# Layer 0, step one in source order with in-place tiles; four of nine channel blocks stored in one pixel order and gathered for the right-hand side

## The chip, the cores and the metric

The kernel runs on one NeuronCore of one Trainium2 chip. The metric is the device time of one launch in microseconds, from three runs of the same program, and beside them one execution was recorded by the hardware profiler. The core has five instruction queues: PE (matmuls; its weight loads, PEld, overlap them), DVE (vector), ACT (scalar, activation functions), POOL (GpSimd) and SP (here it only issues transfers). Transfers (DMAs) are issued from SP, ACT or POOL and carried out by 16 shared DMA engines.

## What is computed

Four residual layers act on an image batch of 8 x 56 x 56 pixels x 192 channels. Only layer 0 is touched by the change. It is a gated token mixer: two projections `q` and `v` to 576 channels are multiplied, the product is convolved along the width with one set of 576 Toeplitz filters and along the height with another, the sum is gated by a third projection `p`, and projected back to 192 channels.

```python
p = silu(x @ p_w.T + p_b)
q = silu(x @ q_w.T + q_b)
v = silu(x @ v_w.T + v_b)
...
qv = q * v
o1 = _toeplitz(qv.reshape(b * h, w, D1), a1).reshape(b, h, w, D1)
o2 = _toeplitz(transpose(qv, (0, 2, 1, 3)).reshape(b * w, h, D1), a2)
...
return (p * (o1 + o2)) @ o_w.T + o_b
```

`x` is group-normalised before it enters, and the result is added to the un-normalised `x`. Everything is float32.

## The kernel before

Layer 0 runs in two steps, with HBM between them.

**Step one** (lines 1319 to 1362 drive it; `layer0_qv`, line 374, is its body) makes `qv` for all eight images. An image lies in SBUF as 128 partitions: the upper and lower 64 partitions hold the two halves of the image (s = 0 and 1), 64 channels to a half, three channel groups j, 1568 pixels each. Per image there are 14 turns (`PH`), each on two pixel rows of either half, 112 pixels, and in a turn the 576 output channels are taken in two pieces of 288 (n). For each piece: 12 matmuls (2 projections x 3 j x 2 halves; each shows as four records of 288 columns, since float32 is passed four times), then for either half one DVE addition of the bias out of PSUM (line 393, 576 elements for q and v together), one ACT Silu (line 394), and one DVE multiplication q*v into a tile `qv` (line 395). After a turn's pieces, SP writes each half's product to HBM **twice**: to `left` (line 398, one DMA, rows of a channel block ordered by pixel row h, content along w) and to `right` (line 403, two DMAs, rows ordered by pixel column w, content along h). Channels are stored in nine blocks of 64 (`NSUB`), so every piece that is written is a run of 64 floats, 256 bytes: 1008 runs in each `left` DMA, 504 in each `right` DMA, and there are 224 and 448 of these DMAs.

Between turns `between[i]` runs small steps of other work: the Toeplitz coefficients (`toeplitz_rows`; PE, DVE), the Toeplitz matrices themselves (128 DMAs in all, `row` and `zeros`, lines 296 and 301, each 9 rows of 14,336 bytes from HBM to HBM, issued from ACT's queue), a bias-and-mask table for layer 1, and at turn 4 the statistics and the normalisation of the next image (`layer0_in`: 12 `bn_stats`, a group sum through PE, ACT Sqrt, and line 371, which writes a normalised copy `xn` of the whole image on DVE). The order of instructions on each engine is the tile framework's scheduler's. `act` has 4 buffers, `qv` 3, `x0` and `xn0` 2 each, PSUM 4 tiles of two banks.

**Step two** (`layer0_mix`, line 521) walks over 72 blocks (8 images x 9 channel blocks). For each it loads two operands into 128 partitions (`layer0_block`, line 409): `lt`, whose even partitions hold 64 rows of the Toeplitz matrix and whose odd ones hold the 64 rows of `left`; and `rt`, the same from `right` with the places swapped, so that one matmul with 128 contraction rows adds both convolutions. Each operand is 128 rows of 14,336 bytes, one DMA on SP's queue (line 417). They have two buffers each (`raws`, bufs=2), so the load of a block is issued when the last copy out of the block two before has been made. From `lt`, POOL copies slices of eight channels (`lc`, line 425), from `rt` DVE and ACT take turns (`rc`); PE multiplies (`op`, line 433), DVE and ACT take the result out (`o`, line 590). Blocks 0 to 3, 4 to 7 and 8 of an image form three passes; the gating and output projection of one pass (lines 438 to 519) is spread between the products of the next. Around block 4 to 5 of each image SP also stores the finished image (line 538) and loads a new one (line 528).

Every DMA is tied to one of eight completion semaphores of the hardware queues (SP and ACT share them), and an issue waits until the DMA that used its semaphore before has landed: at most eight are outstanding.

Of the kernel before, what the change touches and what calls it, by code (L numbers as in the profile page):

```python
# [10 lines left out]
F32 = mybir.dt.float32  # L11
AF = mybir.ActivationFunctionType
ALU = mybir.AluOpType
# [4 lines left out]
B, H, W, C = 8, 56, 56, 192  # L18
NT = H * W
HC = 96  # L20
TT = 392
NTT = NT // TT
D1 = 576
DCH = [(0, 128), (128, 128), (256, 128), (384, 128), (512, 64)]
NSUB = D1 // 64

PASSES = [((0, 1), (0, 1, 2, 3)), ((2, 3), (4, 5, 6, 7)), ((4,), (8,))]
DPERM = [128 * c + 32 * (s % 4) + i for cs, ss in PASSES[:2] for s in ss for c in cs for i in range(32)]
# [22 lines left out]
QR = 56 * 64  # L51
# [11 lines left out]
NH = NT // 2  # L63
NTH = NH // TT
PH = NPAIR // 2
# [24 lines left out]
def kernel(ctx: ExitStack, tc: tile.TileContext, a: dict, out: bass.AP):  # L90
    nc = tc.nc
    nimg = a["x"].shape[0]

    const = ctx.enter_context(tc.tile_pool(name="const", bufs=1))
    dram = ctx.enter_context(tc.tile_pool(name="dram", bufs=1, space=DRAM))
# [17 lines left out]
    gmath = resident("gmath")  # L113
# [7 lines left out]
    eps5 = const.tile([128, 1], F32, name="eps5")  # L121
# [12 lines left out]

    coef = [dram.tile([NSUB, 111, 64], F32, name=f"coef{i}") for i in range(2)]
    none = dram.tile([QR], F32, name="none")
    left, right = (dram.tile([(nimg * W + 64) * NSUB, QR], F32, name=n) for n in ("left", "right"))
    qv_row = lambda b, s: (b * NSUB + s) * W
    toep_row = lambda s: nimg * NSUB * W + 64 * s
    x1 = [dram.tile([C, NT], F32, name=f"x1_{b}") for b in range(nimg)]  # L140
    bmask = dram.tile([8, 128, 3 * 4 * 2 * WN], F32, name="bmask")
    wgd = dram.tile([128, 3, 3 * C], F32, name="wgd")
# [11 lines left out]
    def gn_piece(st, x, t):  # L154

        for j in range(3):
            nc.vector.bn_stats(st[:, j, t], x[:, j, bass.ts(t, TT)])

    def gn_aggregate(st, mv):
        nc.vector.bn_aggr(mv, st.rearrange("p j t s -> p (j t s)"))  # L160
# [29 lines left out]
    def run(steps):  # L190
        for _ in steps:
            pass
# [34 lines left out]
    def toeplitz_rows(psum, pool, rows):  # L227
# [16 lines left out]
        k = 1  # L244
        while k < 55:
            n = min(k, 55 - k)
# [9 lines left out]
        for i in range(2):  # L256
            m = f"m{i + 1}_"
            h = pool.tile([32, 111], F32, name=f"h{i}")
# [3 lines left out]
        for l in range(3):  # L262
            yield
            for i in range(2):
                ps = psum.tile([128, 2, 512], F32, name="hps", tag="qv")
# [6 lines left out]
        for c, (d0, M) in enumerate(DCH):  # L272
            yield
            cos = []
            for i in range(2):
                ps = psum.tile([128, 2, 512], F32, name="aps", tag="qv")
# [7 lines left out]
            for i in range(2):  # L284
                ps = psum.tile([128, 2, 512], F32, name="cps0", tag="qv")
# [4 lines left out]
        zero = pool.tile([128, QR // 128], F32, name="zero", bufs=1)  # L290
        nc.gpsimd.memset(zero, 0.0)
        nc.scalar.dma_start(none.rearrange("(p n) -> p n", p=128), zero)
        parts = [z[toep_row(0):].rearrange("(s k) n -> k s n", k=64) for z in (left, right)]

        def row(i, w0):
            nc.scalar.dma_start(
                parts[i][w0], coef[i][:, 55 - w0:111 - w0].rearrange("s l d -> s (l d)")
            )

        def zeros(i, k):  # L300
            nc.scalar.dma_start(parts[i][k], none.partition_broadcast(NSUB))

        rows += [lambda i=i, k=k: zeros(i, k) for i in range(2) for k in range(W, 64)]
        rows += [lambda i=i, w0=w0: row(i, w0) for i in range(2) for w0 in range(W)]
# [48 lines left out]
    def layer0_load(b, pool):  # L353
        x = pool.tile([128, 3, NH], F32, name="x0")
        nc.gpsimd.dma_start(x, a["x"][b])
        return x

    def layer0_in(b, x, pool, psum):

        sc, sh = scsh[:, 0, b:b + 1], scsh[:, 1, b:b + 1]  # L360
        st = pool.tile([128, 3, NTH, 6], F32, name="gh_st")
        for t in range(NTH):
            gn_piece(st, x, t)
        mv = pool.tile([128, 1, 2], F32, name="gh_mv")
        gn_aggregate(st, mv[:, 0])
        run(gn_finish(mv, sc, sh, pool, psum, "qv"))
        xn = pool.tile([128, 3, NH], F32, name="xn0")
        n = NH if b else TT
        for t in range(NH // n):
            ts = bass.ts(t, n)  # L370
            nc.vector.tensor_scalar(xn[:, :, ts], x[:, :, ts], sc, sh, ALU.mult, ALU.add)
        return xn

    def layer0_qv(b, xn, pool, psum, w_qv, b_qv, between):

        lv, rv = (
            z[qv_row(b, 0):qv_row(b, 0) + NSUB * W].rearrange("(s h) (w d) -> s h w d", h=W, d=64) for z in (left, right)
        )
        for i in range(PH):
            qv = pool.tile([2 * W, 2, D1], F32, name="qv", bufs=3)  # L380
            for n in range(2):
                ns = slice(n * D1 // 2, (n + 1) * D1 // 2)
                ps = [psum.tile([2 * W, 2, 512], F32, name=f"qv{s}", tag="qv") for s in range(2)]
                for which in range(2):
                    for j in range(3):
                        for s in range(2):
                            nc.tensor.matmul(  # L387
                                ps[s][:, which, 0:D1 // 2], xn[64 * s:64 * s + 64, j, bass.ts(i, 2 * W)],
                                w_qv[64 * s:64 * s + 64, j, which, ns], start=(j == 0), stop=(j == 2),
                            )  # L390
                for s in range(2):
                    act = pool.tile([2 * W, 2, D1 // 2], F32, name="act", bufs=4)
                    nc.vector.tensor_tensor(act, ps[s][:, :, 0:D1 // 2], b_qv[:, :, ns], ALU.add)  # L393
                    nc.scalar.activation(act, act, AF.Silu)  # L394
                    nc.vector.tensor_tensor(qv[:, s, ns], act[:, 0], act[:, 1], ALU.mult)
            for s in range(2):
                h0 = H // 2 * s + 2 * i
                nc.sync.dma_start(
                    lv[:, h0:h0 + 2].rearrange("s h w d -> (h w) s d"),
                    qv[:, s].rearrange("t (s d) -> t s d", d=64),  # L400
                )
                for r in range(2):
                    nc.sync.dma_start(
                        rv[:, :, h0 + r].rearrange("s w d -> w s d"),
                        qv[r * W:(r + 1) * W, s].rearrange("w (s d) -> w s d", d=64),
                    )
            for step in between[i]:
                step()

    def layer0_block(b, s, raws):  # L410


        raw = [raws.tile([128, QR], F32, name=n) for n in ("lt", "rt")]
        rows_qv, rows_t = qv_row(b, s), toep_row(s)
        for t, z, even, odd in ((raw[0], left, rows_t, rows_qv), (raw[1], right, rows_qv, rows_t)):
            one = z[even:even + 64]
            nc.sync.dma_start(
                t, bass.AP(one.tensor, one.offset, [[QR, 64], [(odd - even) * QR, 2], [1, QR]]),
            )
        return raw  # L420

# [900 lines left out]
    with ExitStack() as st:  # L1322
        pool = st.enter_context(tc.tile_pool(reuse_waits="tile", name="qv", bufs=2))
        psum = st.enter_context(tc.tile_pool(reuse_waits="tile", name="qvp", bufs=4, space=PSUM))
        w_qv = resident("w_qv", nc.scalar, pool)
        b_qv = pool.tile([2 * W, 2, D1], F32, name="b_qv", bufs=1)
        nc.scalar.dma_start(b_qv.rearrange("p a d -> p (a d)"), a["b_qv"].partition_broadcast(2 * W))
        tz = st.enter_context(tc.tile_pool(reuse_waits="tile", name="tz", bufs=2))
        x = layer0_load(0, pool)
        xn = layer0_in(0, x, pool, psum)  # L1330
        rows, masks = [], []
        coefs, bias = toeplitz_rows(psum, tz, rows), build_bias_mask(psum, tz, masks)
        centred = layer1_weights(tz, psum)

        def pop(todo, n=1):
            for _ in range(min(n, len(todo))):
                todo.pop(0)()

        for b in range(nimg):

            between = {i: [lambda i=i: pop(rows, 2 if i % 3 == 1 else 1)] for i in range(PH)}
            if b == 0:
                for i in range(PH):
                    between[i].insert(0, lambda: [next(coefs, None) for _ in range(2)])
                between[10].append(lambda: next(bias, None))
            elif b == 1:
                between[6].append(lambda: next(bias, None))
                between[12].append(lambda: pop(masks))
            elif b == 2:
                for i in range(6):  # L1350
                    between[2 * i].append(lambda: next(centred, None))
            if b:
                between[9].append(lambda: pop(masks))
            ahead = []
            if b + 1 < nimg:
                x = layer0_load(b + 1, pool)
                between[4].append(lambda: ahead.append(layer0_in(b + 1, x, pool, psum)))
            layer0_qv(b, xn, pool, psum, w_qv, b_qv, between)
            xn = ahead[0] if ahead else None
        pop(rows, len(rows))  # L1360
        pop(masks, len(masks))
    with ExitStack() as st:
        pool = st.enter_context(tc.tile_pool(reuse_waits="tile", name="mix", bufs=2))
# [7 lines left out]
        images, x = ExitStack(), []  # L1371
# [312 lines left out]
```

## Time and profile before

| what | before |
|---|---|
| median of 3 runs | 5757.5 us (5750.73 to 5760.37) |
| the profiled execution: device time, span | 5770.6 us, 5768.8 us |
| mean granted TensorE clock | 0.957 |
| busy share of the span | PE 90%, DVE 58%, ACT 38%, POOL 25% |
| step one: first and last matmul record of line 387 | 28.6 and 846.7 us |
| step one: last store issued (line 403) | 857.2 us |
| step two: last load of an operand issued (line 417) | 1987.0 us |
| transfers: packets, of them under 512 B | 721,922 and 486,376 |

The page's header gives the span; the table of groups gives for each source line how often an instruction ran, the mean of one, and what the engine waited for in front of it; a window row gives the busy time of each engine in a stretch, the clock granted to TensorE, the mean busy share of the 16 DMA engines and what they moved. Step one takes the first 15% of the span and step two the next 20%; the other three layers follow, and the change does not touch them.

### The profile page before, as it was taken

How to read it: one execution, taken by the hardware profiler on the slowest of the kernel's cores; microseconds unless marked ns; L12 is line 12 of the kernel's file. 1: busy time of each engine (PE TensorE's matmuls, PEld its weight loads, DVE VectorE, ACT ScalarE, POOL GpSimd, SP SyncE). 2: the span in 40 equal slices, each digit the busy share in tenths (PEclk: the TensorE clock that was granted, in tenths of full speed). 3: DMA queues.
4: the chain of work that ended last, by engine and by line, in shares of the span. 5: the costliest groups of instructions: out<-in, count | busy, mean ns of one | idle time of the engine just before them, and what ended most of it. 6: DMA issues, size and time to landing. Idle time of an engine off the chain costs nothing. (4 is left out here: it accounts for less than half of the span.)

```text
span 5768.8 us, 116138 instructions
## 1 busy us (share of the span) xinstructions
PE 5181.2 (90%) x50342; PEld 3376.1 (59%) x50342; DVE 3336.5 (58%) x4710; ACT 2169.1 (38%) x2908; POOL 1420.2 (25%) x1107
## 2 busy tenths in 40 slices
PE   6898998999899979999997989999788798999999
PEld 4568765666666645555554657676344597444444
DVE  5777774555555546566665868888778202433331
ACT  2333443333333423333332004555476400433333
POOL 2100004444444424433342013333101101100100
PEclk8999999999999989999998989999899899999999
DMA  6888986776677633222222866666687598212211
GB/s 179 204 211 216 206 182 258 264 264 258 247 262 264 222 92 82 69 75 76 69 65 76 260 235 218 227 232 209 160 232 215 222 328 295 78 62 77 76 41 26
DMA packets 721922, 1013.94 MB, mean 176 GB/s; under 512 B 486376, under 2 KB 645444, under 8 KB 694644
## 3 DMA queue, kind: packets, MB, share of 16 engines
q1 hardware_dynamic: 706352, 940.12, 52.4%
q0 software_dynamic: 8512, 40.62, 2.1%
q10 hardware_dynamic: 6548, 25.78, 1.4%
q8 instruction: 396, 6.49, 0.5%
q14 instruction: 114, 0.93, 0.0%
HBM read 676.92 MB, written 345.97 MB: 177 GB/s over the span
## 5 line engine op out<-in xcount | busy, mean ns | idle before, releaser
L387 PE MATMUL qv<-w_qv_sb,xn 64*112 64x288 f32 x5376 | 711.3, 421 | 48.6 <-DVE act L393 45.4
L425 POOL COPY lc<-lt 128x896 f32<-128x896 f32 (+1 forms) x320 | 552.5, 1751 | 640.9 <-PE op L433 543.1
L387 PEld LDWEIGHTS qv<-w_qv_sb,xn 64*112 64x112 f32 x5376 | 558.5, 182 | 195.5 <-DVE act L393 58.1
L394 ACT ACTIVATE act<-act 112x576 f32<-112x576 f32 x448 | 300.6, 683 | 466.8 <-DVE act L393 427.4
L433 PE MATMUL op<-rc,lc 128*56 128x56 f32 x9216 | 339.1, 221 | 102.1 <-POOL lc L425 64.9
L433 PEld LDWEIGHTS op<-rc,lc 128*56 128x56 f32 x9216 | 307.8, 135 | 177.9 <-POOL lc L425 103.5
L1289 PE MATMUL ph<-y,w_sb 64*128 64x392 f32 x2304 | 397.7, 497 | 6.5 <-ACT hid L1293 6.5
L1300 PE MATMUL po<-hid,w_sb 128*64 128x392 f32 x2304 | 386.3, 494 | 0.0
L393 DVE TENSOR_TENSOR act<-qv,b_qv 112x576 f32<-112x576 f32 x448 | 320.7, 752 | 92.7 <-PE qv L387 92.4
L1307 DVE TENSOR_TENSOR x<-x,z 128x392 f32<-128x392 f32 x96 | 67.0, 698 | 524.2 <-ACT z L1305 524.2
L425 ACT COPY rc<-rt 128x896 f32<-128x896 f32 (+1 forms) x160 | 256.3, 1606 | 249.7 <-PE op L433 227.2
L805 PE MATMUL qk_ps<-xr,wg 64*96 64x392 f32 x1536 | 334.2, 538 | 1.8 <-DVE xr L752 1.7
L1016 PE MATMUL cv<-zc,wt 128*128 128x224 f32 x1536 | 313.6, 356 | 24.2 <-DMA zc<-pd 24.2
L1016 PEld LDWEIGHTS cv<-zc,wt 128*128 128x128 f32 x1536 | 291.0, 190 | 67.5 <-issue 51.2
L1289 PEld LDWEIGHTS ph<-y,w_sb 64*128 64x128 f32 x2304 | 220.0, 188 | 175.9 <-issue 25.5
L445 PE MATMUL pj<-xn,w_p_sb 64*128 64x392 f32 x1536 | 309.8, 511 | 12.4 <-DVE xn L533 8.2
L1190 PE MATMUL cps<-zc,wt 128*128 128x224 f32 x1536 | 300.2, 356 | 18.2 <-DMA zc<-zd 16.8
L1190 PEld LDWEIGHTS cps<-zc,wt 128*128 128x128 f32 x1536 | 289.6, 189 | 28.7 <-issue 21.3
L466 PE MATMUL y<-pp,w_o_sb 128*64 128x392 f32 x1536 | 285.9, 501 | 4.8 <-DVE x L474 4.1
L459 DVE TENSOR_TENSOR pp<-pp,ot 128x784 f32<-128x784 f32 x128 | 124.2, 970 | 284.8 <-ACT pp L450 272.9
L1300 PEld LDWEIGHTS po<-hid,w_sb 128*64 128x64 f32 x2304 | 162.7, 137 | 213.8 <-issue 213.8
L1031 POOL TENSOR_TENSOR rows<-rows,loc 128x896 f32<-128x896 f32 x96 | 220.8, 2300 | 261.7 <-ACT rows L1027 201.9
(233 smaller groups left out, 8895.1 us busy)
## 6 DMA issues: line engine op xcount, KB each, us to landing
lt<-left SPq DMA_DIRECT2D x72, 1792.0 KB
rt<-right SPq DMA_DIRECT2D x72, 1792.0 KB
left<-qv SPq DMA_DIRECT2D x224, 252.0 KB
right<-qv SPq DMA_DIRECT2D x448, 126.0 KB
wt<-in_band_dram SPq DMA_DIRECT2D x23, 2048.0 KB
wt<-in_band_dram SPq DMA_DIRECT2D x11, 4096.0 KB
zc<-pd SPq DMA_DIRECT2D x187, 232.0 KB
pd<-pt SPq DMA_DIRECT2D x7, 5568.0 KB
```

The source lines that it names most:

```text
L387: nc.tensor.matmul(ps[s][:, which, 0:D1 // 2], xn[64 * s:64 * s + 64, j, bass.ts(i, 2 * W)], w_qv[64 * s:64 * s + 64, j, which, ns], start ...
L393: nc.vector.tensor_tensor(act, ps[s][:, :, 0:D1 // 2], b_qv[:, :, ns], ALU.add)
L394: nc.scalar.activation(act, act, AF.Silu)
L425: copy(c[:, 0:nu], raw.rearrange("p (w u d) -> p u d w", u=nu, d=64 // nu)[:, :, d0:d0 + 8])
L433: nc.tensor.matmul(op[64 * u:64 * u + W, i, :], lc[:, u, i], rc[:, u, i], start=True, stop=True)
L445: nc.tensor.matmul(ps[0:M, s, 0:TT], w_p[64 * s:64 * s + 64, j, d0:d0 + M], xn[64 * s:64 * s + 64, j, ts], start=(j == 0), stop=(j == 2),)
L466: nc.tensor.matmul(y[64 * s:64 * s + 64], w_o[0:M, c, 64 * j:64 * j + 64], pp[0:M, s], start=(c == gated[0][0]), stop=(c == gated[-1][0]),)
L805: nc.tensor.matmul(in_pairs(ps[s]), wg[64 * s:64 * s + 64, j, c0:c0 + HC], in_slots(xr[64 * s:64 * s + 64], (3 * g + j) * GW), start=(j == ...
L1016: nc.tensor.matmul(dst, wt[:, c4 + i, 128 * q:128 * q + 128], zc[:, :, c4 + i, q:q + NPAIR], start=(q == 0), stop=(q == 1),)
L1190: nc.tensor.matmul(dst.rearrange("p (b n) -> p b n", n=NPAIR), wt[:, c4 + i, q * OP:(q + 1) * OP], zc[:, :, c4 + i, q:q + NPAIR], start=(q ...
L1289: nc.tensor.matmul(ps[:, s, 0:TT], w0[64 * s:64 * s + 64, j, m * 128:(m + 1) * 128], y[64 * s:64 * s + 64, j, ts], start=(j == 0), stop=(j ...
L1300: nc.tensor.matmul(ps[64 * s:64 * s + 64], w1[:, m, 64 * j:64 * j + 64], hid[:, m, s], start=(m == 0), stop=(m == 5),)
```

## The change

- **Order.** Step one is recorded in a manual schedule: PE, ACT, DVE and POOL run their instructions in the order of the source. SP stays with the scheduler. The steps between are spread over 28 half turns; the statistics of the next image come one `bn_stats` at a time from the eighth half turn on.
- **In place.** The normalised image overwrites `x` (no `xn`); for images 1 to 7 this is done on POOL in four pieces of 1176 elements per partition. q*v overwrites its own `act` tile (no `qv` tile); `act` has 14 buffers. The multiplication comes one half turn late, for half s = 0 on DVE, for s = 1 on POOL.
- **Pieces.** A turn's channels are cut at a block border: 320 (blocks 0 to 4) and 256 (blocks 5 to 8). Each piece is stored as soon as it is multiplied, so a turn's half has two `left` DMAs (560 and 448 runs of 256 bytes) and four `right` DMAs.
- **Kept blocks.** `right` holds only the even channel blocks, five of nine (`KEPT`): its DMAs carry 168 or 112 runs. For an odd block, `rt` is filled by two DMAs: 64 Toeplitz rows of 14,336 bytes, and a gather from `left` of 64 columns x 56 rows, 3,584 runs of 256 bytes.
- **Queue.** The 128 Toeplitz DMAs are issued from SP instead of ACT.

```diff
+KEPT = (NSUB + 1) // 2
...
-    left, right = (dram.tile([(nimg * W + 64) * NSUB, QR], F32, name=n) for n in ("left", "right"))
+    left, right = (
+        dram.tile([nimg * W * k + 64 * NSUB, QR], F32, name=n) for n, k in (("left", NSUB), ("right", KEPT))
+    )
...
         def row(i, w0):
-            nc.scalar.dma_start(
+            nc.sync.dma_start(
                 parts[i][w0], coef[i][:, 55 - w0:111 - w0].rearrange("s l d -> s (l d)")
             )
...
-            nc.scalar.dma_start(parts[i][k], none.partition_broadcast(NSUB))
+            nc.sync.dma_start(parts[i][k], none.partition_broadcast(NSUB))
...
+        for t in range(NTH):
+            xs = x[:, :, bass.ts(t, TT)]
+            (nc.gpsimd if b else nc.vector).tensor_scalar(xs, xs, sc, sh, ALU.mult, ALU.add)
...
+        def multiply(i, s0, s1, acts):
+            n = 64 * (s1 - s0)
+            for s in range(2):
+                eng = (nc.vector, nc.gpsimd)[s]
+                eng.tensor_tensor(acts[s][:, 0, 0:n], acts[s][:, 0, 0:n], acts[s][:, 1, 0:n], ALU.mult)
+            for s in range(2):
+                h0 = H // 2 * s + 2 * i
+                qv = acts[s][:, 0, 0:n].rearrange("t (s d) -> t s d", d=64)
+                nc.sync.dma_start(lv[s0:s1, h0:h0 + 2].rearrange("s h w d -> (h w) s d"), qv)
+                kept = range(s0 + s0 % 2, s1, 2)
+                for r in range(2):
+                    nc.sync.dma_start(
+                        rv[kept[0] // 2:kept[-1] // 2 + 1, :, h0 + r].rearrange("s w d -> w s d"),
+                        qv[r * W:(r + 1) * W, kept[0] - s0:kept[-1] + 1 - s0:2],
+                    )
+
         for i in range(PH):
-            qv = pool.tile([2 * W, 2, D1], F32, name="qv", bufs=3)
-            for n in range(2):
+            for at, (s0, s1) in enumerate(((0, 5), (5, NSUB))):
...
+                acts = [pool.tile([2 * W, 2, 320], F32, name="act", bufs=14) for _ in range(2)]
                 for s in range(2):
-                    act = pool.tile([2 * W, 2, D1 // 2], F32, name="act", bufs=4)
-                    nc.vector.tensor_tensor(act, ps[s][:, :, 0:D1 // 2], b_qv[:, :, ns], ALU.add)
-                    nc.scalar.activation(act, act, AF.Silu)
-                    nc.vector.tensor_tensor(qv[:, s, ns], act[:, 0], act[:, 1], ALU.mult)
...
+                for step in later:
+                    step()
+                later = [lambda now=(i, s0, s1, acts): multiply(*now)]
+                for step in between[2 * i + at]:
+                    step()
+        later[0]()
...
+        )[0:2 - s % 2]:
             one = z[even:even + 64]
...
+        if s % 2:
+            one = left[rows_qv:rows_qv + W]
+            nc.sync.dma_start(raw[1][1:128:2], right[rows_t:rows_t + 64])
+            nc.sync.dma_start(
+                raw[1][0:128:2].rearrange("w (h d) -> w h d", d=64),
+                bass.AP(one.tensor, one.offset, [[64, 64], [QR, H], [1, 64]]),
+            )
...
+        st.enter_context(tc.manual_schedule(
+            engines={mybir.EngineType.PE, mybir.EngineType.Activation, mybir.EngineType.DVE, mybir.EngineType.Pool}
+        ))
+        next(coefs)
+        next(bias)
+        run(layer0_in(0, x, pool, psum))
```

In the order of the built program, POOL has the 42 small loads of the bias table (line 317 before) and the load of image 1 in front of its first multiplication; SP has the loads of the first two blocks of step two among the stores of the last image.

## The prediction

> **What bounds the kernel now.** I read the window rows of step one first: which engine is full, and where.
>
> ```profile
> core 0: us, PE busy (x) PEld busy (x) DVE busy (x) ACT busy (x) POOL busy (x), PEclk, DMA share, GB/s
> 28.00:150.00 122.00, 95.52 (x598) 71.80 (x600) 79.80 (x164) 33.55 (x48) 24.91 (x44) 0.82 0.65 158
> 350.00:450.00 100.00, 89.78 (x690) 65.95 (x686) 66.35 (x120) 38.82 (x57) 1.07 (x2) 0.96 0.92 234
> 750.00:848.00 98.00, 97.07 (x802) 71.72 (x798) 78.72 (x136) 44.87 (x68) 0.60 (x2) 1.00 0.88 180
> ...
> 1450.00:1600.00 150.00, 134.79 (x1852) 90.25 (x1849) 82.14 (x103) 57.01 (x56) 68.38 (x40) 0.98 0.68 254
> ```
>
> At the end of step one PE is full (97 of 98 us, clock 1.00, 802 records); the rows of images 6 and 7, 679 to 765 and 765 to 848 us, give 86 and 83 us per image. Earlier it is not: 690 records in 100 us while the DMA engines are 92% busy, 598 in 122 us in the first image. So step one is bound by the transfers and the start, then by PE. In step two PE idles 15 of 150 us with DMA at 0.68.
>
> Next, what SP pays to issue: by line (min/median/max ns), then in order of time.
>
> ```profile
> L398 SPq DMA_DIRECT2D left<-qv x224: 309/540/5503, 41.6 to 854.9; - x112
> L403 SPq DMA_DIRECT2D right<-qv x448: 418/888/5427, 42.0 to 857.2; - x150
> L296 ACTq DMA_DIRECT2D left<-coef x56: 687/689/712, 134.2 to 383.7; - x56
> L1005 SPq DMA_DIRECT2D zc<-pd x187: 319/443/6851, 3421.1 to 4004.2; - x187
> ```
>
> ```profile
> 756.04 0.31 SPq L398 DMA_DIRECT2D left<-qv  x1
> 756.39 1.56 SPq L403 DMA_DIRECT2D right<-qv  x2
> 758.05 0.66 SPq L398 DMA_DIRECT2D left<-qv  x1
> 758.75 1.73 SPq L403 DMA_DIRECT2D right<-qv  x2
> ```
>
> A store issued after a pause takes 0.31 us; in a row they take more, with 0.04 to 0.10 us between, and the three stores of one half of the image in a turn take 2.0 to 2.5 us of SP: 224 x 2.5 = 560 us, hidden because SP has 820.
>
> Third, who waits in step two (waited for: us, times, longest), and POOL's copies in time.
>
> ```profile
> PE op L433 <- POOL lc L425: 64.9, 65, 2.4
> POOL lc L425 <- DMA lt<-left: 62.7, 14, 11.1
> PE op L433 <- DVE rc L425: 12.5, 6, 7.3
> ```
>
> ```profile
> 1467.27 1.80 POOL L425 COPY lc<-lt 128x896 f32<-128x896 f32 x1 [0.16 <-PE op L433]
> 1470.88 6.48 POOL L425 COPY lc<-lt 128x896 f32<-128x896 f32 x3 [1.82 <-DMA lt<-left]
> 1478.56 2.86 POOL L425 COPY lc<-lt 128x896 f32<-128x896 f32 x1 [1.20 <-PE op L433]
> 1481.57 2.29 POOL L425 COPY lc<-lt 128x896 f32<-128x896 f32 x1 [0.16 <-DMA lt<-left]
> ```
>
> PE waits for `lc`, and POOL starts a block's `lc` the moment `lt` lands: loads there have no slack. Block 1 of an image is the exception: its `rt`, issued at 1430.9, is first copied at 1458.7 us.
>
> **The change, part by part.**
>
> *Stores: fewer bytes.* Runs of 256 B fall from 224 x 1008 + 448 x 504 = 451,584 to 225,792 + 448 x (168 + 112) = 351,232. Price of a run: in 750 to 848, 0.88 x 98 x 16 = 1380 engine-us moved 180 GB/s x 98 us = 17.6 MB = 68,900 runs, 20 ns. So the DMA engines lose 100,352 x 0.020 / 16 = 125 us of work over step one, 0.15 of its span, and stop being the limit.
>
> *Stores: more issues.* SP issues 448 `left`, 896 `right` and, moved from ACT, 128 Toeplitz DMAs: 1472 for 672. Whatever a DMA carries, each has an issue price. `left`: 0.31 (pause) to 0.54 (median under load); I take 0.44, the median of line 1005, a plain store-sized issue in a row, + 0.05 for the gap. `right`: 0.418 to 0.888; the median was paid with full DMA engines and 504 runs, so I stay near the least: 0.46 + 0.05. Toeplitz: 0.69 + 0.05, line 296. Sum 448 x 0.49 + 896 x 0.51 + 128 x 0.74 = 220 + 457 + 95 = 772 us, against PE's own 8 x 83 = 664. SP becomes the bound, and 14 `act` buffers (seven half turns) only delay PE's feeling it. Start: SP's third store needs POOL's first multiplication, behind the 42 small loads that end at 46.7 us now; SP is productive from about 45. Image loads: 2.35 MB is 8 rows of 18.8 kB per engine, some 6 us in which a store lands later, without slack on SP: I book 2 us, 8 times, 16. Last store: 45 + 772 + 16 = 833 us, now 857: **-24**. With the least prices (0.36, 0.47, 0.74) it is 45 + 677 + 16 = 738 (-119); with `right` at 0.55, the first one after a `left` above, and `left` at 0.54, + gap: 264 + 538 + 95 + 61 = 958 (+101). Every 0.01 us of an issue is 13 us.
>
> The Trainium skill, "DMA: Bandwidth & Descriptors", section "Issuing engines are not separate DMA queues", speaks against booking the moved Toeplitz issues at all: spreading issues over queues saves only sequencer time, usually small beside the transfer. Line 296's 0.69 us is no smaller than what its nine rows cost an engine (0.61 us each, below); by the rule the sum would lose its 95 us and PE would nearly be the bound, by the row it stands.
>
> *DVE, ACT, POOL.* Per image DVE has 56 additions x 0.752 (line 393) = 42, 28 multiplications x about 0.46 (line 395) = 13, 12 statistics x 0.554 = 7: 62 us of some 98, hidden. It loses 224 x 0.46 and seven whole-image normalisations of 2.73. ACT: 56 x 0.683 = 38, hidden; it loses 128 issues. POOL's multiplications from line 1214 (448 elements 936 ns, 1344 2704 ns, so 0.05 + 1.97 ns each): 0.68 and 0.56 us, 17 us an image, plus four normalisation pieces of some 1.4 us (line 1135: 1568 elements 1.84): hidden. In-order waiting is covered by the half turn's delay and seven half turns of buffers; without that cover each late item costs its own length. The next image's load has seven half turns (24 us) before its first `bn_stats`; landing took 11.5 us.
>
> DVE's copy in step two (line 425, rc) takes 539 ns at best and 2890 at worst beside POOL's copies. The Trainium skill, "SBUF — State Buffer", section "Who interferes with whom", says why to expect that here too: a DVE instruction with two SBUF inputs and a POOL one that reads SBUF exclude each other for a whole instruction. By it each DVE product could stand 0.68 us longer, 28 x 0.68 = 19 us an image; 81 of 98 us is still hidden.
>
> *Gather.* An even block keeps its 8 rows of 14,336 B per DMA engine; price of a row: in 1450 to 1600, 0.68 x 150 x 16 = 1632 engine-us for 38.1 MB, 0.61 us, so 4.9 us. An odd `rt` has 4 rows (2.46) and 224 runs. The trace has no gathered read of 256 B. Lower bound: at the rows' rate, 11 ns each, 2.5 us: no loss. Upper: the mask loads, 49 pieces of 196 B deep, land 5.6 us after issue against 2.1 for the 28-byte loads beside them, 71 ns each: 15.9 us, +13.5 a block. I take the store's 20 ns, same size, stride and memories: 4.5 us, **+2.0** per odd block. Block 1 hides it; blocks 3, 5, 7 of 8 images don't (what queues behind it on the same engines is the next `lt`, then `lc`, then PE): 24 x 2.0 = 48, some absorbed where `lt` has a few us: **+40**. SP's issue of 3,584 runs may hold it some us; nothing due is behind it for 3 us.
>
> Sum: -24 + 40 = **+16**: 5768.8 to about 5785 us of span. The median runs are 11.3 us below that span: 5757.5 + 16 = 5774.
>
> **Rivals.**
>
> *A. Issues are cheap, PE becomes the bound.* For: 0.31 and 0.418 do occur. Against: in a row neither line shows them often; medians are 0.54 and 0.89. With the least prices step one ends at 738 (PE alone: 28.6 + 664 + about 20 for the first image = 713): -119 + 40 = -79: 5678. It is faster as soon as an issue costs below about 0.50 us on average, gap included.
>
> *B. Gathered reads are dear.* For: small reads of the mask. Against: these are not 256 B aligned. Halfway, 40 ns: 9.0 + 2.5 = 11.5 us, +6.6 a block, now exposed in 28 of 32 blocks: +185 - 24 = +161: 5918. It decides alone from 16 ns on, where 24 exposed blocks cost the 24 us won.
>
> *C. Issues dear*, as in the sum above: 958, +101 + 40: 5898.
>
> **The numbers.** The sum as worked out 0.46, A 0.34, B 0.12, C 0.08. A difference under 0.2% (11.5 us) cannot be told from none. The likeliest case lies +16 with its own range 5740 to 5810, so it is slower (0.30), same (0.14) or faster (0.02); with B and C slower 0.50, with A faster 0.36. Range for 8 in 10: down to A's end, 5680, up to 5860, short of the ends of B and C.
>
> **What would show it.** Step one right: last store near 833 us, SP's stores back to back in images 1 to 6 with about 0.5 us each, PE idle before line 387 because of PSUM held by additions that wait for `act`. A right: 83 us per image, PE over 95% busy. Gather right: odd `rt` lands 2 us later than an even one, POOL and DVE wait for loads about 40 us more in all, image period of step two up from (2045 - 854) / 8 = 149 to 154 us. I am wrong if SP pauses in images 1 to 6, or if step two keeps its length.

## The result and the profile after

The changed kernel takes **5952.4 us** (median of four runs, 5947.0 to 5955.6) against 5757.2 (5750.7 to 5760.4): a ratio of 1.034, 95% interval 1.0322 to 1.0358. The forecast was 5774, with a range that ended at 5860. The profiled execution has a span of 5945.2 us, 176 longer than before.

Where the 176 us lie can be read from one DVE instruction that runs once an image in step two, the normalisation `xn`. A group's line gives min/median/max in ns and then the start of the first and the last; the kernel before stands first, the changed one second.

```profile
L533 DVE TENSOR_SCALAR xn<-x,scsh x8: 2728/2730/3357, 870.2 to 1929.7; 128x4704 f32<-128x4704 f32 x8
```

```profile
L577 DVE TENSOR_SCALAR xn<-x,scsh x8: 2728/2729/2730, 927.5 to 2099.8; 128x4704 f32<-128x4704 f32 x8
```

The first `xn` comes 57 us later: that is step one. From the first to the last, seven images of step two, it is 1172.3 us for 1059.5, so **167.5 us an image for 151.4**: 113 us more. Behind the last `xn` 6 us are lost. Both steps became slower.

**Step one.** A window row of its middle, of the kernel before and then of the changed one (the 5376 records of step one stand for 2688 matmuls, two for each and not four):

```profile
core 0: us, PE busy (x) PEld busy (x) DVE busy (x) ACT busy (x) POOL busy (x), PEclk, DMA share, GB/s
400.00:600.00 200.00, 175.30 (x1338) 160.44 (x1336) 142.75 (x263) 79.74 (x117) 1.07 (x2) 0.92 0.89 218
```

```profile
400.00:600.00 200.00, 175.01 (x1218) 132.97 (x1216) 116.41 (x201) 73.30 (x108) 57.52 (x69) 0.92 0.69 160
```

SP's stores in the changed kernel, by line and then in order of time:

```profile
L412 SPq DMA_DIRECT2D left<-act x448: 309/350/3307, 41.8 to 917.3; - x150
L415 SPq DMA_DIRECT2D right<-act x896: 307/465/4056, 42.2 to 918.2; - x180
```

```profile
500.14 0.31 SPq L412 DMA_DIRECT2D left<-act  x1
500.50 0.95 SPq L415 DMA_DIRECT2D right<-act  x2
501.55 0.34 SPq L412 DMA_DIRECT2D left<-act  x1
501.94 0.95 SPq L415 DMA_DIRECT2D right<-act  x2
502.93 0.73 SPq L301 DMA_DIRECT2D right<-coef  x1
```

What the engines waited for between 200 and 900 us (us in total, times, longest):

```profile
DVE act L433 <- DMA right<-act: 190.6, 121, 10.8
PEld qv L427 <- DVE act L433: 124.0, 96, 8.3
PE qv L427 <- DVE act L433: 83.8, 50, 7.7
```

The DMA engines fell from a share of 0.89 to 0.69 in this stretch, as forecast, yet PE got only 1218 records into 200 us, for 1338. The chain is in the waits: an addition has no free `act` tile because a store has not landed, PSUM stays held, PE stands. The last store is issued at 918.2 us, for 857.2. Summed over the issue records between the first store and the last, SP spends 749.6 us inside issues, 89.2 in pauses below 0.2 us between them, and 38.0 in longer ones: it is full. An `act` tile's first store leaves about 21 us after its addition, and from image 1 on some 12 of the 14 tiles hold products whose stores are not all issued.

**Step two.** TensorE's rows between the last products of block 4 and the first of block 5 in one image, before and then after (start, duration; 128*56 names products, 64*128 and 56*128 the gate):

```profile
1355.97 1.04 PE L433 MATMUL op<-rc,lc 128*56 128x56 f32 x32
1356.94 2.25 PE L445 MATMUL pj<-xn,w_p_sb 64*128 64x392 f32 x12
...
1371.74 1.04 PE L433 MATMUL op<-rc,lc 128*56 128x56 f32 x32 [0.38 <-DVE rc L425]
```

```profile
1468.98 0.99 PE L477 MATMUL op<-rc,lc 128*56 128x56 f32 x28
1469.90 1.59 PE L489 MATMUL pj<-xn,w_p_sb 64*128 64x392 f32 x8
...
1484.46 2.25 PE L489 MATMUL pj<-xn,w_p_sb 64*128 64x392 f32 x12 [0.80 <-ACT pp L494]
...
1496.42 2.25 PE L489 MATMUL pj<-xn,w_p_sb 64*128 64x392 f32 x12 [0.80 <-ACT pp L494]
...
1502.06 1.90 PE L477 MATMUL op<-rc,lc 128*56 128x56 f32 x64
```

Before, the gate's work between them lasts 15 us, after, 32, and in those 32 us nothing else runs on PE. It is not the data that is late: the gather for this block is issued at 1460.96 us, its last part lands at 1479.5, and the first copy out of `rt` starts 21 us later:

```profile
1500.55 1.83 DVE L469 COPY rc<-rt 128x896 f32<-128x896 f32 x2
```

The instructions stand in another **order**. Step two is not in a manual schedule; the framework's scheduler places its instructions, and with the gather in the program 214 records of the gate's matmuls and transposes stand between these products of images 1 to 6 instead of 102 (149 and 73 instructions, as the expectations below count them). Why the gather makes it choose so, no run shows; a likely reason is that it counts on later data. The gate alone goes at 12 us a pixel piece, through `pj`, Silu, multiplication, `y`, and less of it is left to fill the gaps between the later products: PE's wait for `lc` between 1000 and 2000 us rose from 55.6 to 77.7 us.

### The profile page after: what moved, and what is told of

It is laid out like the page before. It is cut to its first block, busy times and chain, and to the rows that moved or that the text cites. A ratio compares the mean times of both kernels' runs of the same rounds, so it can differ in the third digit from the quotient of the medians.

```text
span 5945.2 us, 118162 instructions
## 1 busy us (share of the span) xinstructions
PE 5265.4 (89%) x50342; PEld 3417.8 (57%) x50342; DVE 3216.9 (54%) x4479; ACT 2159.1 (36%) x2908; POOL 1610.2 (27%) x1359
## 5 line engine op out<-in xcount | busy, mean ns | idle before, releaser
L427 PE MATMUL qv<-w_qv_sb,x 64*112 64x320 f32 (+1 forms) x5376 | 757.0, 424 | 98.3 <-DVE act L433 93.5
L469 POOL COPY lc<-lt 128x896 f32<-128x896 f32 (+1 forms) x320 | 526.1, 1677 | 798.7 <-PE op L477 789.3
L427 PEld LDWEIGHTS qv<-w_qv_sb,x 64*112 64x112 f32 x5376 | 585.6, 182 | 259.3 <-DVE act L433 144.3
L433 DVE TENSOR_TENSOR act<-qv,b_qv 112x640 f32<-112x640 f32 x448 | 327.5, 753 | 352.5 <-DMA right<-act 209.9
L437 ACT ACTIVATE act<-act 112x640 f32<-112x640 f32 x448 | 297.6, 683 | 543.2 <-DVE act L433 466.1
L489 PE MATMUL pj<-xn,w_p_sb 64*128 64x392 f32 x1536 | 332.6, 524 | 64.2 <-ACT pp L494 36.8
L408 POOL TENSOR_TENSOR act<-act 112x320 f32<-112x320 f32 x224 | 178.6, 797 | 576.9 <-ACT act L437 492.6
L510 PE MATMUL y<-pp,w_o_sb 128*64 128x392 f32 x1536 | 323.2, 517 | 4.1 <-DVE x L518 4.1
L894 POOL TENSOR_TENSOR e<-e,mx 128x1176 f32<-128x1176 f32 x64 | 139.9, 2187 | 561.0 <-DVE mx L893 497.5
```

The lines of the kernel that those rows point to most:

```text
L427: nc.tensor.matmul(ps[s][:, which, 0:n], x[64 * s:64 * s + 64, j, bass.ts(i, 2 * W)], w_qv[64 * s:64 * s + 64, j, which, 64 * s0:64 * s1], ...
L433: nc.vector.tensor_tensor(acts[s][:, :, 0:n], ps[s][:, :, 0:n], b_qv[:, :, 64 * s0:64 * s1], ALU.add)
L437: nc.scalar.activation(acts[s][:, :, 0:n], acts[s][:, :, 0:n], AF.Silu)
L469: copy(c[:, 0:nu], raw.rearrange("p (w u d) -> p u d w", u=nu, d=64 // nu)[:, :, d0:d0 + 8])
L489: nc.tensor.matmul(ps[0:M, s, 0:TT], w_p[64 * s:64 * s + 64, j, d0:d0 + M], xn[64 * s:64 * s + 64, j, ts], start=(j == 0), stop=(j == 2),)
L510: nc.tensor.matmul(y[64 * s:64 * s + 64], w_o[0:M, c, 64 * j:64 * j + 64], pp[0:M, s], start=(c == gated[0][0]), stop=(c == gated[-1][0]),)
```

## The experiments

Image times below are from `xn` as above, (last - first) / 7. The expectations count an image from its first right-hand copy on DVE, which takes in image 0 and with it the end of step one; that count is the second column of images.

| kernel | program us | last store | image, `xn` | image, first copies |
|---|---|---|---|---|
| before | 5757.2 | 857.2 | 151.4 | 147.9 |
| changed | 5952.4 | 918.2 | 167.5 | 165.6 |
| rows_act | 5971.7 | 927.2 | 167.9 | 166.3 |
| all_kept | 5846.3 | 926.7 | 152.7 | 148.1 |
| mix_order_before | 5858.0 | 859.8 | 161.8 | 161.8 |
| mix_order_after | 5925.7 | 919.2 | 164.1 | 166.0 |
| old_order_gather | 5845.7 | 914.9 | 153.3 | 151.2 |
| new_order_plain | 5978.3 | 930.6 | 166.8 | 163.3 |
| turn_stores | 5796.5 | 752.7 | 168.2 | 166.4 |
| turn_all_kept | 5737.3 | 802.7 | 153.7 | 149.0 |
| right_act | 5936.7 | 902.9 | 167.8 | 164.2 |
| rows_pool | 5952.3 | 900.6 | 169.3 | 167.4 |
| turn_split | 5949.0 | 916.8 | 168.5 | 168.4 |
| turn_old_order | 5683.3 | 753.4 | 153.1 | 151.5 |

From rows_act on, each time but turn_old_order's is that of one execution; differences of some 10 us between these are not read.

### Step two: the order or the gather

**all_kept.** Step one as changed, but all nine blocks stored on the right.

```diff
-KEPT = (NSUB + 1) // 2
+KEPT = NSUB
...
-        )[0:2 - s % 2]:
+        ):
...
-        if s % 2:
-            one = left[rows_qv:rows_qv + W]
-            nc.sync.dma_start(raw[1][1:128:2], right[rows_t:rows_t + 64])
-            nc.sync.dma_start(
...
```

> The changed kernel with all nine channel blocks of the right operand stored in both orders (KEPT = 9) and plain loads as before, no gather; step one in order and in place as changed, with the same number of stores, larger by 9/5 in bytes on the right. Theory (step one is bound by the number of issues, step two lost its time to another order of its instructions, which follows from the gather): the last store stays within 905 to 930 us, an image of step two takes 149 us as before the change, the program 5945 - 8 x 15 = about 5825. Rival 1 (step one is bound by bytes): last store beyond 950. Rival 2 (step two is slow because of step one's new placement or the in-place tiles, not because of the gather): an image stays at 164 us and the program near 5945.

The image is back at 152.7 us, and so is the order: as in the kernel before, 102 of the gate's records stand between the last products of block 4 and the first of block 5. Rival 2 falls. The last store moves by 8.5 us only, although the right-hand stores carry 9/5 of the bytes: rival 1 falls too. (The program lay 21 us above the theory's figure: the first `xn` comes at 945.6 us, 18 us later than in the changed kernel.)

**mix_order_before** and **mix_order_after.** The order of step two as written, without and with the gather.

```diff
-        layer0_mix(pool, blocks, psum, ops, w_p, w_o, loaded)
+        with tc.manual_schedule(
+            engines={mybir.EngineType.PE, mybir.EngineType.Activation, mybir.EngineType.DVE, mybir.EngineType.Pool}
+        ):
+            layer0_mix(pool, blocks, psum, ops, w_p, w_o, loaded)
```

> The kernel before the change, but with the instructions of step two on TensorE, VectorE, ScalarE and GpSimd kept in the order in which they are written, in which the gate's matmuls are spread evenly over the turns of blocks 4 to 7 (20, 20 and 12 between turns). Plain loads, no gather. It is the partner of the next run. An image is expected at 145 to 165 us, against 149; no theory fixes it closer.

> The changed kernel with its gather, and with step two in written order, as in the partner run; so the two have the same order on four engines in step two, and only the gather differs. Theory (the gather cost step two its time by another order, not by its own duration): an image takes within 4 us of the partner's. Rival 1 (the gather's own 2 us per odd block, exposed three times per image, as forecast): 5 to 8 us longer than the partner's. Rival 2 (the gather itself is worth the whole loss): 12 us or more longer.

The written order alone costs 10 us an image with plain loads. With equal order the gather adds 2.3 us (161.8 to 164.1). By first copies it is 4.2, at the edge of the bound, but image 0, which starts at different points of step one, is in that figure. In this order none of the gate's records stand between blocks 4 and 5.

**old_order_gather** and **new_order_plain.** The crosswise pair. Step two's calls are recorded, and issued in the order that the scheduler gave them in the other kernel, in a manual schedule; SP stays with the scheduler.

```diff
+        real, nc = nc, Recorder(nc)
...
+        recorder.replay()
         loaded()
```

> The changed kernel with its gather, its instructions of step two on TensorE, VectorE, ScalarE and GpSimd put in exactly the order that they have in the kernel before the change (there at most 73 of the gate's matmuls and transposes stand ahead of block 5's first products, in the changed kernel 149). Theory (the gather costs step two its time by the other order that came with it; its own duration is worth the 4 us an image that the pair in written order showed): an image takes 148 + 4 = 152 us (149 to 155) against 165.6 in the changed kernel, and the program about 5945 - 8 x 13 = 5840. Rival (the gather's own duration is the loss, and the other order only follows it without harm): an image stays at 160 us or more, the program above 5900.

> The other half: the changed kernel with all nine blocks of the right operand stored and loaded plainly, no gather, but its instructions of step two in the order of the changed kernel. Theory (order): an image takes 158 to 163 us although no gather is there, the program about 5940. Rival (gather's own duration): 148 to 152 us, the program about 5845, as with all nine kept in the order before.

| image, `xn` | plain loads | gather |
|---|---|---|
| order of the kernel before | 152.7 | 153.3 |
| order of the changed kernel | 166.8 | 167.5 |

The order is worth 14 us an image in both columns, the gather 0.6 or 0.7 in both rows; by first copies 14 to 15 and 2 to 3. The traces show the two orders as they should be: 102 records between blocks 4 and 5 of images 1 to 6 in the upper row, 214 in the lower. How far the gather's figures carry, other rows of the table above tell: six runs share the changed kernel's order and gather, and their images take 167.5 to 169.3 us; three share the order and plain loads of before, with 151.4 to 153.7; and turn_old_order, with the gather, lies 0.6 below turn_all_kept, without it. So the order's 14 us are clear, and the gather's cost is not clear of nothing. new_order_plain's image by first copies, 163.3, lies just past the expected 163, and its program time 38 us above the expected one, by its later step one (first `xn` at 958.0 us). The waits between 1000 and 2000 us say the same. POOL's copies of `lc` and PE's `pj`, in the kernel before, in old_order_gather (where replayed calls all carry line 76), in the changed kernel, and in new_order_plain (line 77):

```profile
PE pj L445 <- ACT pp L450: 2.1, 13, 0.2
POOL lc L425 <- PE op L433: 436.2, 123, 13.1
```

```profile
PE pj L76 <- ACT pp L76: 1.9, 12, 0.2
POOL lc L76 <- PE op L76: 471.1, 124, 11.8
```

```profile
PE pj L489 <- ACT pp L494: 27.8, 37, 1.0
POOL lc L469 <- PE op L477: 578.8, 111, 31.4
```

```profile
PE pj L77 <- ACT pp L77: 27.6, 38, 1.0
POOL lc L77 <- PE op L77: 591.2, 115, 31.4
```

PE's wait for the Silu (2 or 28 us) and POOL's longest wait for the products (12 to 13, or 31.4 us) go with the order, whether or not there is a gather.

### Step one: what SP's time is made of

**rows_act.** The Toeplitz rows on ACT's queue again.

```diff
-            nc.sync.dma_start(
+            nc.scalar.dma_start(
                 parts[i][w0], ...
```

> The changed kernel with the 128 Toeplitz row copies (the rows and the zero rows) issued on ScalarE's queue again, as before the change; all else as changed. Theory (step one is bound by SyncE's issuing: 750 us of issues, 89 us of gaps of 0.06 us between them and 38 us of waits make up its 876 us): SyncE loses 128 x (0.76 + 0.06) = 105 us, the last store goes from 918 to about 815, and the program from 5945 to about 5840; step two keeps its 164 us per image. Rival (the stores' bytes or the waits of the additions for their buffers bound step one): the last store stays above 890 us. A third outcome, between the two (830 to 880), says that another engine becomes the bound on the way.

The rival's outcome, but not clean. ACT runs in order, and the issues that now stand among its instructions wait for stores (waits between 200 and 900 us):

```profile
ACT act L437 <- DMA right<-act: 270.1, 69, 13.6
```

In the changed kernel it was 52.1 us in the same stretch. So the Silus came late, and the run says little of SP. The same step on a queue without stores:

**rows_pool.**

```diff
-            nc.sync.dma_start(
+            nc.gpsimd.dma_start(
                 parts[i][w0], ...
```

> The changed kernel with the 128 Toeplitz row copies issued on GpSimd's queue, which no store uses; all else as changed. On ScalarE's queue they had made the Silus wait for the landing of stores (270 us between 200 and 900 us), so that run said nothing of SyncE. Theory (SyncE's issuing bounds step one): SyncE loses 128 x (0.76 + 0.06) = 105 us of its 876, the last store comes at 810 to 840 us, the program at about 5850, step two unchanged at 165 us an image. Rival (what issues is shared by the queues, or the stores' landing bounds): the last store stays above 885 us, and the issues left on SyncE grow longer or SyncE waits for landings.

The last store comes 18 us earlier, not 80 to 105. SP hardly waits; it issues 933 DMAs between 200 and 800 us in 528.6 us, where the changed kernel issued 1038 in 525.0. The issues that are left grew: the mean of a `right` store from 0.52 to 0.62 us, of a `left` store from 0.39 to 0.45, at nearly unchanged medians. Of the 126 us that the stores between 170 and 740 us take above their medians (45 in the changed kernel), 71 fall into the second microsecond after POOL issued a row, 0.43 us a store there. So what SP pays "for issuing" is in part a wait for something behind the queue that the rows occupy, from whichever queue they come. Which part of the path that is, no run shows.

**right_act.** Half of the right-hand stores on ACT's queue.

```diff
-                    nc.sync.dma_start(
+                    (nc.sync, nc.scalar)[r].dma_start(
                         rv[kept[0] // 2:...
```

> The changed kernel with one of the two right-hand stores of each half piece (448 of 896) issued on ScalarE's queue, behind the Silus of the next piece; SyncE keeps 896 stores and the 128 Toeplitz rows. Theory 1 (what is short in step one is issuing as a whole, and two queues share it, as the Toeplitz rows on ScalarE's queue suggested): the stores left on SyncE take longer each, and the last store stays within 880 to 960 us. Theory 2 (SyncE's own instruction stream is short): SyncE is relieved of 448 x 0.54 = 240 us of 840, another engine bounds, and the last store comes at 850 us or earlier.

The time is the first theory's (902.9 us), its sign is not: SP's stores do not grow (`right` 0.50 us in the mean). Instead SP has a wait that is not among its seven largest in the changed kernel, here between 200 and 800 us:

```profile
SPq L412 <- DMA right<-act: 145.3, 99, 8.6
```

With two queues on the same eight completion semaphores a store waits for the landing of the other queue's: 140 of these 145 us are for stores that ACT had issued. The relief became a wait; between the two theories this run does not decide.

**turn_stores** and **turn_split.** Both products of a turn go side by side into one tile; the tile is stored once a turn (672 DMAs), or, in turn_split, cut in two at the border of block 5 (1344 DMAs of the same tiles at the same moments).

```diff
+                    turn[s][:, s0:s1].rearrange("t s d -> t (s d)"), acts[s][:, 0, 0:n], acts[s][:, 1, 0:n], ALU.mult
...
+            if s1 < NSUB:
+                return
...
+                nc.sync.dma_start(lv[:, h0:h0 + 2].rearrange("s h w d -> (h w) s d"), turn[s])
+                for r in range(2):
+                    nc.sync.dma_start(
+                        rv[:, :, h0 + r].rearrange("s w d -> w s d"), turn[s][r * W:(r + 1) * W, 0:NSUB:2],
+                    )
```

> The changed kernel with the products of the two pieces of a turn written side by side into one tile and stored once a turn: 672 stores of the same bytes and runs in place of 1344; act tiles 6 in place of 14; gather and step two as changed. Moving the Toeplitz rows to ScalarE's queue did not help: SyncE's stores took longer each (right 0.52 to 0.62 us in the mean), so two queues seem to share what issues them, and the number of DMAs is what counts. Theory (number of DMAs issued): 672 fewer at 0.48 + 0.06 us = 363 us less of issuing, so another engine bounds step one, TensorE with 176 of 200 us busy at 876 us first; the last store comes between 780 and 850 us, the program at 5945 - 70 to 140, step two unchanged at 165 us an image. Rival (the runs of 256 bytes or the bytes bound step one, which this leaves as they are): last store above 890.

> The kernel with one store a turn, and only this changed: each of its 672 stores is cut into two at the border of block 5, so the same tiles, buffers, bytes and moments, but 1344 DMAs again. Theory (the number of DMAs is what bounds step one in the changed kernel): the last store goes back from 753 to 880 us or later, the program from 5795 to 5920 or more. Rival (the gain came from the turn's own tiles, which let the additions go on while stores are under way, not from the number): the last store stays below 790 us, the program below 5830.

752.7 us with one store, below what was expected, and 916.8 with two, as expected: the **number of DMAs** is what made step one slow, not the bytes, the runs, the tiles or the order. The same window of turn_stores, then of turn_split:

```profile
400.00:600.00 200.00, 200.00 (x1635) 196.95 (x1633) 149.83 (x258) 96.95 (x142) 72.68 (x87) 1.00 0.86 205
```

```profile
400.00:600.00 200.00, 175.08 (x1248) 143.94 (x1246) 110.04 (x202) 75.20 (x110) 57.60 (x70) 0.94 0.68 161
```

With one store a turn PE is the bound, 1635 records instead of 1248, and the DMA share goes up, not down. The price of a DMA did not stay what it was, though. A `right` issue of the whole turn takes 0.90 us in the mean (0.51 in turn_split) and a `left` issue 0.51 (0.41), so 672 DMAs fewer than in the changed kernel took 181 us off SP's issues and short pauses, not the 363 of the expectation; SP still spends 658 of 707 us on them.

### The repairs put together

**turn_all_kept.** One store a turn, all nine blocks, no gather.

> As the run before, with all nine blocks of the right operand stored and loaded plainly, so step two has its order of before and no gather. Theory: last store 790 to 870 us (the DMA engines' share was 0.80 at 927 us with all nine kept, so bytes allow some 740), an image of step two at 148 us, the program 5769 + 12 + (last store - 857), that is 5715 to 5795. Rival (bytes or runs): last store above 900, the program above 5820.

5737.3 us, inside the theory. Against the kernel before it has the same number of stores, the same bytes and the same order in step two; its 54 us in step one (802.7 for 857.2) belong to the rest of the change (written order, normalisation in place, POOL's share of the multiplications, rows on SP), which no run takes apart. Keeping five of nine blocks gives the other 50 (752.7).

**turn_old_order.** turn_stores and old_order_gather together.

> The two repairs together: the changed kernel with one store a turn (672 stores) and with the instructions of step two in the order of the kernel before, with five of nine blocks stored and the gather kept. If the two losses are separate and add up: last store at 753 us as with the turn's stores alone, an image of step two at 151 us as in the order of before, so 5794 - 8 x 15 = about 5677 us (5660 to 5700), faster than the kernel before by 1.2 to 1.8%. If step two's gain needed a late step one, an image takes 155 us or more and the program stays above 5700.

5683.3 us (5675.3 to 5691.1), ratio to the kernel before **0.9871**, interval 0.9852 to 0.9889. Both gains add up: last store 753.4, an image 153.1.

## Why the prediction was wrong

- **"SP becomes the bound"** was right in its marks: SP is back to back in images 1 to 6 (18.5 us of longer pauses from 150 us on), and PE is idle before line 427 because additions wait for `act`. Rival A, cheap issues, is out. But SP's own time is not all that is short: rows_pool took 105 us of issues off it, and the last store came only 18 us earlier.
- **The sum of step one, -24 us, came out at +61.** The term that was mis-sized is `right`: booked at "0.46 + 0.05", near its least, because the 0.888 of before was paid with full DMA engines. Measured over the whole step it is 0.523 + 0.062 of pause, so 896 x 0.585 = 524 us instead of 457: +67. `left` was 0.404 + 0.062 (209 instead of 220), the Toeplitz rows 0.76 + 0.06 (105 instead of 95), start and longer pauses 80 instead of 61. That is 918 instead of 833. The high end of the step's own bounds, 958, held it. The median of a `right` issue came out at 0.465, as booked; a median leaves out the tail that carries the wait behind the queue.
- **"by the row it stands"**, against the rule of the Trainium skill ("DMA: Bandwidth & Descriptors", section "Issuing engines are not separate DMA queues"), was wrong. The 128 rows were booked at 95 us on SP; put on POOL's queue they give back 18 (on ACT's none, but there the Silus waited too). The rule, that all queues end on the same DMA engines and that issuing from several saves only the sequencer's time, agrees with the little that rows_pool gave back. That this time is usually small beside the transfer does not fit here: SP spends 749.6 of 877 us inside issues, while the DMA engines have a share of 0.69 in the row above.
- **"*Gather* ... +2.0 per odd block", +40 us in all, was too dear, not too cheap.** The price of a run was right: the trace of the changed kernel has 3,584 packets of 256 B for each gather, 22 ns each in the mean, where 20 were booked and rival B asked for 40. What was wrong is how much of it stands in anyone's way. With the order held fixed the gather costs 0.6 to 2.3 us an image, 5 to 18 us in all and not clear of nothing, where 5 an image were forecast. Rival B (dear gathered reads) would have come nearest by its time, and for the wrong reason.
- **What failed in step two is a step that was not in the sum at all.** The sentence "what queues behind it on the same engines is the next `lt`, then `lc`, then PE" takes step two's order as given. It was the scheduler's, and the gather changed it: 14 us an image, 99 of the 113 us between the first and the last `xn`. Of the rest the gather has 4; 9 are in all_kept too (152.7 for 151.4), no more than runs with an equal step two differ by. The mark "POOL and DVE wait for loads about 40 us more" told it apart: POOL's wait for `lt` between 1000 and 2000 us fell from 62.7 to 4.6 us, while the image grew by 16.
- DVE, ACT and POOL were hidden in step one, as said. POOL's multiplication took 0.80 us, booked at 0.56 and 0.68, without harm. Beside it the DVE product took 0.56 us in the mean, for 0.46 before: some 3 us an image, where 19 were allowed for.

In spans the forecast was 5785 and the execution 5945: of the 160 us, 81 lie ahead of the first `xn` (+57 for -24), 79 behind it, where 99 and more for the order were missing and the gather was booked too high.

## What to carry to other kernels

Where a scheduler sets the order, compare the order of every engine before and after, also in the stage whose instructions the change leaves alone: here another way to load one operand moved work of another kind, although the load came in time. Cutting stores into more and smaller DMAs to start them earlier costs an issue price for each, and this price is not the median of an issue but issue, pause and the wait behind the queue together; moving DMAs to another queue gave little of it back. The mean DMA share does not show this: step one waited for its stores at 0.69, and reached 0.86 with half as many DMAs.

## What the runs showed of the hardware

- In the middle of step one PE was granted a clock of 1.00 with 200 of 200 us busy (turn_stores), and of 0.92 and 0.94 with 175 (changed, turn_split). It is no rule of the busy share alone: between 1000 and 1200 us, in step two of the changed kernel, it is 0.99 with 173 of 200 us busy. Over all of step one the mean record went from 424 to 406 ns, and the time in which any of these matmuls runs from 757 to 678 us. So removing the waits was worth more than the waits: turn_stores' 753 us lies below the 780 to 850 that was expected from PE's busy share. How much of this is the clock, no run separates.
- A load that is issued soon after a gather of 3,584 runs stands in its issue. In the changed kernel, next to the gather for block 5, behind the load of an image:

```profile
1459.97 0.33 SPq L572 DMA_DIRECT2D x<-in_x_dram  x1
1460.41 0.50 SPq L459 DMA_DIRECT2D rt<-right  x1
1460.96 0.73 SPq L460 DMA_DIRECT2D rt<-left  x1
1467.82 9.35 SPq L454 DMA_DIRECT2D lt<-left  x1
1477.27 0.55 SPq L454 DMA_DIRECT2D rt<-right  x1
```

In old_order_gather, behind a gather without an image load:

```profile
1226.08 0.59 SPq L553 DMA_DIRECT2D rt<-left  x1
1228.76 5.86 SPq L76 DMA_DIRECT2D lt<-left  x1
```

The gather's own issue takes 0.73 us, the next load's 9.35, for 0.51 elsewhere. Both long issues end some 8 us (gather alone) and 16 us (with the image load) behind the gather's; in the changed kernel loads that come 6 us or more behind a gather alone take 0.51 in most cases, and behind the image load alone, in the kernel before, the next loads take 0.55 to 0.58:

```profile
1353.52 0.33 SPq L528 DMA_DIRECT2D x<-in_x_dram  x1
1353.95 0.55 SPq L417 DMA_DIRECT2D rt<-right  x1
1354.59 0.56 SPq L417 DMA_DIRECT2D lt<-left  x1
1355.25 0.58 SPq L417 DMA_DIRECT2D rt<-right  x1
```

Nothing was due behind the long issue of the changed kernel.
